# Criss-cross attention and a Fourier mixer: the norm's parts later in each block's iteration, and one small copy on another engine

## The chip, the cores and the metric

The kernel runs on one NeuronCore of a Trainium2 chip. Its engines work from queues of their own: TensorE (PE in the profile, its weight loads PEld), VectorE (DVE), ScalarE (ACT), GpSimd (POOL) and SyncE (SP, which here only starts transfers). An engine takes its instructions in order and waits on semaphores that other engines raise. The metric is the time of one execution in device microseconds, the median of several runs. Before the change it is 3218.33 us (3213.28 to 3226.0 in three runs).

## The reference

The input x has 8 images of 128 x 128 pixels with 64 channels, in fp32. Layer 0 is attention along the column and the row of every pixel, layer 1 a Fourier mixer with a small convolution:

```python
energy_H = jnp.einsum('bhwd,bkwd->bhwk', Q, K)      # Q, K: 8 channels
energy_H = jnp.where(diag, -jnp.inf, energy_H)
energy_W = jnp.einsum('bhwd,bhvd->bhwv', Q, K)
att = jax.nn.softmax(jnp.concatenate([energy_H, energy_W], axis=-1), axis=-1)
x = gamma[0] * (out_H + out_W) + x                  # layer 0
h = _pw(_ln(x, g1, b1), w_te, b_te)                 # layer 1
F = jnp.fft.fft2(h.astype(jnp.complex64), axes=(1, 2))
...
x1 = x + _pw(sp, w_tp, b_tp)
...
return x1 + _pw(d, w_fp, b_fp)
```

The norm that this case speaks of is the first `_ln` of layer 1: mean and variance over the 64 channels of each pixel. The kernel computes it at the end of the attention stage.

## The kernel before, in words

**Stages.** `attention` handles layer 0 for all 8 images and writes for each image the result x2 and the normed, transposed result xn to DRAM. `mixer` reads both and computes layer 1. In the profiled execution the attention stage takes some 1250 of 3220 us; the mixer begins with PE at 1277.

**Blocks.** An image is worked in 8 blocks: four H blocks (32 columns each, attention along the height), then four W blocks (32 rows each, attention along the width). Called H0 to H3 and W0 to W3 here, they make 64 tasks. The loop of line 618 runs over n and is a software pipeline: in iteration n, block n+1 is loaded into PE's layout and gets its queries, keys, values and first energies (to find the maxima), block n gets its shifted energies, exponentials and half of its attend products, and block n-1 the other half. The later work on a W block follows further behind: the weights that merge the two directions (`weigh`, `total`) one iteration after, `invert` and the merge (`combine`) two after, the sums of the norm (`norm_step` with m = n - 4) four after, and the inverse root and the scaling (`norm_step` with m = n - 5, part 3) five after. As an image has four H blocks after the previous image's four W blocks, the norm's sums of an image's W blocks fall into the H iterations of the next image. Those of the last image fall into four iterations after the last block.

**Order.** PE, ACT, DVE and POOL take their instructions in the order in which the loop writes them (`manual_schedule`, line 617). SP's order is made by the framework from the dependencies.

**One iteration on PE:** transposes of block n+1 (L367), attend of n-1 (L422) with the transpose of the maxima (L410), queries and keys (L381), attend of n-1, values (L400), energies of both blocks for two quarters (L452, with mask matmuls L444 in H iterations), values, two attends of n, energies for the other two quarters. All products go to four PSUM buffers of one ring, so each new product waits until an older one has been read: by ACT (xt L371, qt L388, the exponentials L463, the outputs y L428, 128x520 each) or by DVE (shift L411, kt L391, v L403, the negated maxima m L457). Three of the ring's waits matter here: the second pair of energies waits for v, the second values wait for the first maxima, and the next block's transposes for the third maxima.

**The norm's parts.** `norm_step(n, part)` works on half a block (16 rows of 64 channels on 128 partitions, 1024 elements). Part 0 squares the first half on ACT (L578) and sums the rows on DVE (L579); part 1 sums the squares on DVE (L581); parts 2 and 3 do the same for the second half. Part 3 also starts `inverse_root` on POOL for the block before (17 small instructions, lines 88 to 104), and for every second block the scaling of two blocks into `z` (L593, 8 instructions) and the transfer of `z` to xn in DRAM (L597, 2 MB, issued by POOL). Only near the end of the last image do the roots, scalings and squares run on DVE (`merger`; L576).

**The merge.** `combine` is on POOL: 16 instructions of 128x512 (L560 and L563) and the store of x2 (L564). It reads yh, the outputs of the H blocks of its image (one buffer, used for all images), and yw, the outputs of two W blocks (two buffers, `target`, line 489). The squares of part 0 and 2 and `z` are written into the yw buffer of their blocks, so the buffer is free for a later pair only when L597 has read it.

**The maxima.** `maximum(n)` keeps the negated maxima of an H block in `mh` (128x32 of 128x128), which is transposed on PE when the image's H blocks are done (L514); for a W block it starts the weights on POOL (L503). The input was written in the iteration before.

Of the kernel before, what the change touches and what calls it, by code (L numbers as in the profile page):

```python
# [260 lines left out]
def attention(tc, nc, x, w_q, b_q, w_k, b_k, w_v, b_v, gamma, x2, xn, prm, marks, packed, thirds):  # L261
    NB = x.shape[0]
    with ExitStack() as ctx:
# [166 lines left out]
        def energies(a, k, new, old, masked):  # L430


            jobs = []
            if new is not None:
                e1 = ps.tile([P, 2, 4, P], F32, tag="ps", name="e1")
                jobs += [(e1, q, 2 * k + q, new.qt, new.kt, False) for q in range(2)]
            if old is not None:
                e2 = ps.tile([P, 2, 4, P], F32, tag="ps", name="e2")
                jobs += [(e2, q, 2 * (1 - k) + q, old.kt, old.qt, masked) for q in range(2)]
                if masked:  # L440
                    for t in range(4):
                        for q in range(2):
                            rows = slice(32 * (2 * (1 - k) + q), 32 * (2 * (1 - k) + q) + 32)
                            nc.tensor.matmul(  # L444
                                e2[:, q, :, 32 * t : 32 * t + 32], lhsT=mleft[rows, t, :],
                                rhs=mright[rows, :].unsqueeze(1).to_broadcast([32, 4, 32]),
                                start=t == 0, stop=False,
                            )
            for j in range(4):
                for e, q, quad, left, right, msk in jobs:  # L450
                    rows = slice(32 * quad, 32 * quad + 32)
                    nc.tensor.matmul(  # L452
                        e[:, q, j, :], lhsT=left[rows, 4 * a + j, :], rhs=right[rows, 4 * a + j, :],
                        start=not msk, stop=j == 3 or not msk,
                    )
            if new is not None:
                nc.vector.tensor_reduce(  # L457
                    new.mneg[:, 2 * k : 2 * k + 2, 4 * a : 4 * a + 4],
                    e1, AX.X, ALU.max, negate=True,
                )  # L460
            if old is not None:
                att = p4.tile([P, 2, 4, P], F32, tag="att", name="att", bufs=5)
                nc.scalar.activation(att, e2, AF.Exp)  # L463
                old.att[a, 1 - k] = att
# [8 lines left out]
        def begin(n):  # L473
            b, way, blk = tasks[n]
            if way == "H":
                if blk == 0:
                    o = img[b] = Image()
                    o.mh = p2.tile([P, P], F32, tag="mh", name="mh")
                    o.mdt = late.tile([P, 2, P], F32, tag="mdt", name="mdt")
            state[n] = Block(n, loaded.pop(n))  # L480
# [13 lines left out]
        def maximum(n):  # L494

            b, way, blk = tasks[n]
            s, o = state[n], img[b]
            cols = slice(blk * R, blk * R + R)
            if way == "H":
                nc.vector.tensor_copy(o.mh[:, cols].rearrange("p (q i) -> p q i", q=4), s.mneg)  # L500
                return
            t = s.t = late.tile([P, 5, R], F32, tag="tsm", name="tsm", bufs=4)
            nc.gpsimd.tensor_tensor(  # L503
                t[:, 0, :].rearrange("p (q i) -> p q i", q=4),
                o.mdt[:, 0, cols].rearrange("p (q i) -> p q i", q=4), s.mneg, ALU.subtract,
            )
# [12 lines left out]
        def merger(n):  # L519

            return nc.vector if n >= len(tasks) - 3 else nc.gpsimd
# [5 lines left out]
        def is_w(n):  # L527
            return 0 <= n < len(tasks) and tasks[n][1] == "W"
# [37 lines left out]
        def norm_step(n, part):  # L566


            m = n - 4
            if is_w(m):  # L570
                s = state[m]
                h = slice(16 * (part // 2), 16 * (part // 2) + 16)
                sq = s.y[:, h, 0:C]
                if part % 2 == 0:
                    if m >= N - 3:
                        nc.vector.tensor_tensor(sq, s.xb[:, h, :], s.xb[:, h, :], ALU.mult)  # L576
                    else:
                        nc.scalar.activation(sq, s.xb[:, h, :], AF.Square)  # L578
                    nc.vector.tensor_reduce(s.t[:, 0, h], s.xb[:, h, :], AX.X, ALU.add)  # L579
                else:  # L580
                    nc.vector.tensor_reduce(s.t[:, 1, h], sq, AX.X, ALU.add)  # L581
            m = n - 5
            if is_w(m):
                b, way, blk = tasks[m]
                s = state[m]
                r, q, t = (s.t[:, i, :] for i in range(3))
                if part == 3:
                    inverse_root(merger(m), m >= N - 3, r, q, t)
                if part == 3 and blk % 2 == 1:
                    z = s.yw.rearrange("p r c -> p (r c)")[:, 0 : 2 * R * C].rearrange("p (c r) -> p c r", c=C)  # L590
                    for o, lo in ((state[m - 1], 0), (s, R)):
                        for h in range(0, R, 8):
                            merger(m).tensor_tensor(  # L593
                                z[:, :, lo + h : lo + h + 8].rearrange("p c r -> p r c"), o.xb[:, h : h + 8, :],
                                o.t[:, 0, h : h + 8].unsqueeze(2).to_broadcast([P, 8, C]), ALU.mult,
                            )
                    (nc.sync if m >= N - 3 else nc.gpsimd).dma_start(out=xn[b][:, blk // 2, :, :], in_=z)  # L597
# [8 lines left out]
        def flush(n):  # L606
            for _ in range(n):
                if later:
                    later.pop(0)()
# [7 lines left out]
        with tc.manual_schedule(engines={E.PE, E.Activation, E.DVE, E.Pool}):  # L617
            for n in range(-1, N + 6):
                for m in (n + 2, n + 3):
                    if m >= 2 and m < N and (m == n + 2) == (tasks[m][1] == "H"):  # L620
                        fetch(m)
                new = old = last = None
                masked = False
                if n + 1 < N:
                    begin(n + 1)
                    new = state[n + 1]
                    new.turn()
                flush(1)
                if 0 <= n < N:
                    old = state[n]  # L630
                    masked = tasks[n][1] == "H"
                    moved = lambda yp: old.shift(yp[:, 0, 384:512])
                if 0 <= n - 1 < N:
                    last = state[n - 1]
                    last.attend(1, 1, last.y, moved if old is not None else None)
                elif old is not None:
                    moved(ps.tile([P, 2, 512], F32, tag="ps", name="mt"))
                if new is not None:
                    new.queries()
                norm_step(n, 0)  # L640
                if last is not None:
                    last.attend(1, 0, last.y)
                    across_all(n - 1)
                if old is not None:
                    maximum(n)
                if new is not None:
                    new.values(0)
                flush(1)
                norm_step(n, 1)
                if is_w(n - 2):  # L650
                    invert(n - 2)
                if new is not None or old is not None:
                    for k in range(2):
                        energies(0, k, new, old, masked)
                norm_step(n, 2)
                if is_w(n - 1):
                    weigh(n - 1)
                if new is not None:
                    new.values(1)
                if old is not None:  # L660
                    target(n)
                    old.attend(0, 1, old.y)
                    old.attend(0, 0, old.y)
                flush(1)
                if new is not None or old is not None:
                    for k in range(2):
                        energies(1, k, new, old, masked)
                if is_w(n - 1):
                    total(n - 1)
                norm_step(n, 3)  # L670
                if is_w(n - 2):
                    combine(n - 2)
                if 0 <= n < 4:
                    prepare[n]()
                state.pop(n - 7, None)
                flush(1)
# [711 lines left out]
```

## Time and profile before

| | |
|---|---|
| median of three runs | 3218.33 us (3213.28, 3218.33, 3226.0) |
| profiled execution | 3221.41 us, span 3219.6 us |
| busy: PE, PEld, DVE | 2944.8 (91%), 2142.9 (67%), 2548.9 (79%) us |
| busy: ACT, POOL | 2100.1 (65%), 1561.0 (48%) us |
| granted TensorE clock | 0.971 |
| DVE sums of the norm, L579 and L581 | 64 each, median 1207 and 1206 ns |
| ACT squares, L578 | 58, median 1058 ns |
| DVE copy of the maxima, L500 | 32, 169 / 531 / 1159 ns (least, median, most) |
| POOL transfer L597 | 14 of 2048 KB, 9.4 us from issue to landing |

How to read it: busy shares are means over a stage of attention and a stage of mixing with different limits, so what happens in the attention stage is read from its own stretches. In the lines of the prediction, a time line gives the start, the duration in us, the engine, the line of the kernel, the operation, output and inputs, the number of instructions merged, and in brackets the idle time of the engine before it and what ended that. "issue" is idle time for which the profile shows no releaser. The granted clock is a share of TensorE's full clock.

### The profile page before, as it was taken

The numbers are of one execution on the slowest core, as the hardware profiler recorded it, in microseconds if no ns is written. First come the engines' busy times: TensorE is split into PE (matmuls) and PEld (weight loads), VectorE is DVE, ScalarE is ACT, GpSimd is POOL, SyncE is SP. The second block draws the span as 40 slices with busy tenths as digits, with TensorE's granted clock in tenths as the row PEclk, the third lists the DMA queues.
The fourth block names the chain that finished last, engine by engine and source line by source line (L and its number), as shares of the span: only waits on it lengthen the run. The fifth ranks groups of instructions, "written<-read, shape, count | busy, mean of one in ns | idle before, by whom it ended". The sixth has DMA issues, their size and how long they took to land.

```text
span 3219.6 us, 110523 instructions
## 1 busy us (share of the span) xinstructions
PE 2944.8 (91%) x50612; PEld 2142.9 (67%) x50612; DVE 2548.9 (79%) x2322; ACT 2100.1 (65%) x2744; POOL 1561.0 (48%) x1944
## 2 busy tenths in 40 slices
PE   7998888988888987999999899999899999999978
PEld 6877777777777776666576576575566575665644
DVE  4574747474756567719999999999999999999996
ACT  3665656565655655538868768768668678677654
POOL 1095959595958585414515415515415425335321
PEclk8999999999999998999999999999999999999989
DMA  6024242434333323232552653643634634634433
GB/s 174 23 95 129 99 120 95 128 97 136 108 107 120 95 94 135 101 123 40 144 134 50 157 110 66 158 93 73 161 83 89 156 84 93 151 77 81 96 62 75
DMA packets 222458, 339.17 MB, mean 105 GB/s; under 512 B 142879, under 2 KB 176296, under 8 KB 207528
## 3 DMA queue, kind: packets, MB, share of 16 engines
q0 software_dynamic: 32496, 154.84, 20.4%
q1 hardware_dynamic: 188728, 177.19, 19.4%
q8 instruction: 397, 6.50, 0.8%
q14 instruction: 69, 0.57, 0.1%
q10 hardware_dynamic: 768, 0.07, 0.0%
HBM read 137.40 MB, written 102.25 MB: 74 GB/s over the span
## 4 chain that ended last, share of the span: by engine, by line
PE 52%; DVE 33%; issue 6%; POOL 6%; ACT 1%; DMA 1%; SPq 0%; POOLq 0%; DVEq 0%; ACTq 0%
DVE acc L1159 23%; PE yp L422 6%; PE fcps L859 5%; PE e L452 4%; PE dps L927 3%; PE yps L914 3%; PE vps L400 3%; DVE m L457 3%; PE tp L367 3%; PE pq L381 3%; PE yps L916 3%; PE tpy L603 2%; POOL xb L563 2%; PE op L1225 2%; PE aps L819 2%
## 5 line engine op out<-in xcount | busy, mean ns | idle before, releaser
L1159 DVE SCALAR_TENSOR_TENSOR acc<-h,pk,acc 128x1024 f32<-128x1024 f32 x840 | 1332.6, 1591 | 34.8 <-ACT acc L1145 13.3
L875 POOL TENSOR_TENSOR gs<-gl 128x512 f32<-128x512 f32 (+2 forms) x272 | 418.7, 1593 | 245.3 <-ACT gl L869 234.4
L859 PE MATMUL fcps<-f,pk 128*128 128x512 f32 (+2 forms) x1088 | 499.4, 591 | 0.0
L457 DVE TENSOR_REDUCE m<-e 128x8 f32<-128x1024 f32 x256 | 300.9, 1211 | 207.0 <-PE e L452 206.4
L1153 POOL DMA_DIRECT2D acc<-pr x120 | 105.6, 880 | 644.8 <-DVE acc L1159 428.1
L869 ACT ACTIVATE gl<-fcps,pk 128x1024 f32<-128x1024 f32 (+2 forms) x272 | 291.1, 1074 | 118.1 <-PE fcps L859 95.6
L463 ACT ACTIVATE att<-e 128x1024 f32<-128x1024 f32 x256 | 259.7, 1024 | 165.3 <-PE e L452 161.5
L422 PEld LDWEIGHTS yp<-v,att 128*64 128x64 f32 x8192 | 270.3, 143 | 89.1 <-issue 42.2
L1060 POOL TENSOR_TENSOR xc<-x,st 128x512 f32<-128x512 f32 x128 | 183.7, 1440 | 286.5 <-DVE st L101 186.1
L859 PEld LDWEIGHTS fcps<-f,pk 128*128 128x128 f32 x1088 | 190.5, 190 | 197.3 <-issue 162.8
L452 PE MATMUL e<-kt,qt 32*128 32x128 f32 x4096 | 298.4, 288 | 23.8 <-DVE v L403 12.7
L422 PE MATMUL yp<-v,att 128*64 128x65 f32 x8192 | 298.3, 230 | 20.6 <-issue 18.7
L452 PE MATMUL e<-qt,kt 32*128 32x128 f32 x4096 | 297.0, 286 | 15.6 <-issue 13.5
L452 PEld LDWEIGHTS e<-kt,qt 32*128 32x128 f32 x4096 | 257.9, 191 | 44.4 <-issue 21.2
L452 PEld LDWEIGHTS e<-qt,kt 32*128 32x128 f32 x4096 | 255.3, 191 | 20.2 <-issue 13.9
L1149 ACT ACTIVATE pr<-h,pk 128x1024 f32<-128x1024 f32 x176 | 214.1, 1236 | 0.0
L899 PEld LDWEIGHTS gps<-pk,gs 128*64 128x64 f32 x4032 | 135.5, 141 | 116.5 <-issue 65.5
L403 DVE TENSOR_TENSOR v<-vps,bv 128x1024 f32<-128x1024 f32 x128 | 155.9, 1218 | 66.9 <-PE vps L400 66.8
L914 PE MATMUL yps<-tb,gt 128*64 128x128 f32 x1024 | 200.8, 278 | 3.0 <-DVE ot L1230 2.4
L400 PE MATMUL vps<-wv,xt 64*64 64x64 f32 x8192 | 158.9, 228 | 46.6 <-DVE m L457 27.7
L915 PE MATMUL yps<-tb,gt 128*64 128x128 f32 x1024 | 200.8, 278 | 0.0
L842 PE MATMUL fps<-tb,at 128*64 128x128 f32 x1008 | 196.3, 277 | 0.0
(226 smaller groups left out, 7424.5 us busy)
## 6 DMA issues: line engine op xcount, KB each, us to landing
acc<-pr POOLq DMA_DIRECT2D x120, 512.0 KB, 5.4
xb<-in_x_dram SPq DMA_DIRECT2D x32, 1024.0 KB
xn<-xn SPq DMA_DIRECT2D x32, 1024.0 KB
x<-x SPq DMA_DIRECT2D x32, 1024.0 KB
x<-xb POOLq DMA_DIRECT2D x30, 1024.0 KB, 6.0
out_dram<-ot SPq DMA_DIRECT2D x120, 256.0 KB
xn<-yw POOLq DMA_DIRECT2D x14, 2048.0 KB, 9.4
pr<-pr POOLq DMA_DIRECT2D x56, 512.0 KB, 6.4
```

What stands on the lines that cost most here:

```text
L400: nc.tensor.matmul(vps[z, s, j, :], lhsT=self.xts[t][rows, j, z], rhs=wv[rows, :], start=True, stop=True)
L422: nc.tensor.matmul(yq[z, q, j, :], lhsT=att[:, q, j, z], rhs=self.v[:, r, :], start=True, stop=True)
L452: nc.tensor.matmul(e[:, q, j, :], lhsT=left[rows, 4 * a + j, :], rhs=right[rows, 4 * a + j, :], start=not msk, stop=j == 3 or not msk,)
L457: nc.vector.tensor_reduce(new.mneg[:, 2 * k : 2 * k + 2, 4 * a : 4 * a + 4], e1, AX.X, ALU.max, negate=True,)
L463: nc.scalar.activation(att, e2, AF.Exp)
L859: nc.tensor.matmul(ps[:, sgn, 0:n], lhsT=w[:, cols], rhs=fv, start=True, stop=not mean)
L869: nc.scalar.activation(gl[:, :, 0:n], ps[:, :, 0:n], AF.Gelu, bias=bfc[:, half : half + 1])
L875: nc.gpsimd.tensor_tensor(gs[:, 0:n], gl[:, 0, 0:n], gl[:, 1, 0:n], ALU.add if half == 0 else ALU.subtract)
L914: nc.tensor.matmul(yps[0:64, c, :], lhsT=gr, rhs=cosn, start=True, stop=False)
L915: nc.tensor.matmul(yps[64:128, c, :], lhsT=gi, rhs=cosn, start=True, stop=False)
L1149: nc.scalar.activation(pr, self.lines(k, t), AF.Identity, bias=zero, scale=wdw[:, t : t + 1])
L1159: nc.vector.scalar_tensor_tensor(out=a, in0=self.lines(k, t), scalar=wdw[:, t : t + 1], in1=a, op0=ALU.mult, op1=ALU.add)
```

## The change

Part 0 of the norm moves from after the queries to after the first two calls of `energies`, part 1 from before those energies to after the second `values`, and part 2 from before the second `values` to after the last two calls of `energies`. Part 3 stays at the end. In an H iteration the copy of the maxima to `mh` is done by ACT in place of DVE, at the same place of the order.

```diff
             if way == "H":
-                nc.vector.tensor_copy(o.mh[:, cols].rearrange("p (q i) -> p q i", q=4), s.mneg)
+                nc.scalar.copy(o.mh[:, cols].rearrange("p (q i) -> p q i", q=4), s.mneg)
                 return
...
                 if new is not None:
                     new.queries()
-                norm_step(n, 0)
                 if last is not None:
                     last.attend(1, 0, last.y)
                     across_all(n - 1)
...
                 flush(1)
-                norm_step(n, 1)
                 if is_w(n - 2):
                     invert(n - 2)
                 if new is not None or old is not None:
                     for k in range(2):
                         energies(0, k, new, old, masked)
-                norm_step(n, 2)
+                norm_step(n, 0)
                 if is_w(n - 1):
                     weigh(n - 1)
                 if new is not None:
                     new.values(1)
+                norm_step(n, 1)
                 if old is not None:
                     target(n)
                     old.attend(0, 1, old.y)
...
                     for k in range(2):
                         energies(1, k, new, old, masked)
+                norm_step(n, 2)
                 if is_w(n - 1):
                     total(n - 1)
                 norm_step(n, 3)
```

## The prediction

> **What bounds the kernel now.** I read the page first (busy time, shares by slice), then the instructions of single block iterations in order of time, then the chain that ended last, then busy time by stage. The page gives no single bound for the attention stage: TensorE (PE) is busy 7 or 8 tenths in the first sixteen slices, while POOL alternates between full and half.
>
> ```profile
> PE   7998888988888987999999899999899999999978
> POOL 1095959595958585414515415515415425335321
> ```
>
> The block iteration that begins at 350.53 (image 2, second column block, called H1) shows what the change aims at. DVE in order of time:
>
> ```profile
> 355.83 1.23 DVE L391 TENSOR_TENSOR kt<-pq,bk 128x1024 f32<-128x1024 f32 x1 [0.72 <-PE pq L381]
> 356.97 1.21 DVE L579 TENSOR_REDUCE tsm<-xb 128x16 f32<-128x1024 f32 x1
> 358.09 0.88 DVE L500 COPY mh<-m 128x32 f32<-128x32 f32 x1
> 358.90 1.21 DVE L403 TENSOR_TENSOR v<-vps,bv 128x1024 f32<-128x1024 f32 x1
> 360.03 1.20 DVE L581 TENSOR_REDUCE tsm<-yw 128x16 f32<-128x1024 f32 x1
> 361.16 0.34 DVE L547 RECIPROCAL tsm<-tsm 128x32 f32<-128x32 f32 x1
> 361.42 2.28 DVE L457 TENSOR_REDUCE m<-e 128x8 f32<-128x1024 f32 x2
> ```
>
> and PE beside it:
>
> ```profile
> 360.16 0.38 PE L452 MATMUL e<-kt,qt 32*128 32x128 f32 x2 [0.93 <-DVE v L403]
> 362.62 1.16 PE L400 MATMUL vps<-wv,xt 64*64 64x64 f32 x64 [1.29 <-DVE m L457]
> ```
>
> PE stands 0.93 and 1.29 us because v and the maxima queue on DVE behind a norm sum, the copy of the maxima and a second norm sum. So far the change looks worth about 2 us in each of 28 iterations. The chain between two images says otherwise. POOL, from the merge of one image's row blocks (L560, L563) to the transfer of the normed rows (L597):
>
> ```profile
> 312.57 0.25 POOL L541 TENSOR_TENSOR tsm<-mdt,tsm 128x32 f32<-128x32 f32 x1 [12.19 <-ACT tsm L535]
> 404.65 8.12 POOL L593 TENSOR_TENSOR yw<-xb,tsm 128x512 f32<-128x512 f32 x8
> 413.06 0.62 POOL L597 DMA_DIRECT2D xn<-yw  x1 [0.30 <-POOL yw L593]
> ```
>
> and what waits for it on ACT, in images 1, 2 and 5:
>
> ```profile
> 268.98 0.59 ACT L428 COPY yw<-yp 128x520 f32<-128x520 f32 x1 [3.19 <-DMA xn<-yw]
> 422.57 1.09 ACT L428 COPY yw<-yp 128x520 f32<-128x520 f32 x2 [6.71 <-DMA xn<-yw]
> 888.17 0.59 ACT L428 COPY yw<-yp 128x520 f32<-128x520 f32 x1 [4.71 <-DMA xn<-yw]
> ```
>
> POOL's timeline has no gap over 1 us between 312.57 and 413.06: four merges, two inverse roots and one scaling, 100.5 us. The first row block of the next image (W0) writes its outputs into the buffer that this transfer empties (target, line 482, two yw buffers). The page's median landing for L597 is 9.4 us. From its issue to the first W0 copy the seven images take 9.8, 9.5, 13.9, 9.9, 9.7, 12.5 and 9.5 us (issues at 259.17, 413.06, 566.70, 723.15, 878.48, 1032.88, 1189.36). So in five of seven the copy starts as the transfer lands. In images 3 and 6 PE was late instead: 4.84 and 2.29 us of "issue" idle stand before their attend matmuls.
>
> The loop from image to image is then: 12.5 us from the start of W2 to POOL's total, 100.5 on POOL, 9.5 for the transfer, and 31.1 from that copy to the next W2 (453.69): 153.6, which is the distance of the two W2 (300.07 to 453.69). The column blocks H0 to H3, where the change acts, are not in this sum. They run beside POOL:
>
> ```profile
> 332.31:402.77 70.46, 62.84 (x1860) 52.10 (x1861) 56.81 (x54) 45.05 (x56) 64.98 (x93) 1.00 0.31 108
> 402.77:453.69 50.92, 42.43 (x925) 36.04 (x926) 21.49 (x18) 26.59 (x33) 29.25 (x65) 0.93 0.58 168
> ```
>
> (stretch, length, busy PE, PEld, DVE, ACT, POOL, granted clock, DMA share, GB/s; first H0 to H3, then W0 and W1.)
>
> **The change, part by part.** All norm parts act where the block four before is a row block: H0 to H3 of images 1 to 7 (28 iterations), and four iterations after the last block. Parts 0 and 2 are each a Square on ACT (1.06) and a sum on DVE (1.21), part 1 a sum of squares (1.20). None of the three issues anything on POOL or SP and no DMA. Part 3, with the roots, the scaling and L597, stays. So nothing is moved past those two queues.
>
> *Removed from DVE ahead of what PE waits for:* one sum and the copy before v, one sum of squares before the maxima. In the iteration above v could start as its matmuls end, at 357.95 instead of 358.90, and the maxima at 359.3 instead of 361.42. Both idles go: 17.96 - 0.93 - 1.29 = 15.74. An iteration without norm parts is a check: W3 of image 1 takes 15.64, without the column blocks' masks.
>
> *New waits.* (1) The first sum now stands before the second v: DVE from the maxima's end goes 1.21 + 1.21 while PE does vps and two attends (1.16 + 2.09); 0 to 0.3 us. (2) The second Square now stands on ACT between the last exponential and the two xt copies of the next block. The xt copies move back by about 0.85 us; the first has that slack (PE has 3.3 us of other work before the queries), the second not quite: 0.1 to 0.5. (3) A sum and the part-3 sum stand before the shift of qt (L411), which waits for PE until 3.3 us into the iteration; they end at 3.3 us: 0 to 0.1. Together I take 0.3 of 0.1 to 0.9, near the low end since each item has cover: an iteration of 16.0. (4) The copy of the maxima on ACT: no row has ACT doing it; nearest are L533 with 128x32 at 0.22 on ACT and L500 at 0.17 to 1.16 on DVE, so 0.2 to 1.2. I take 0.2, on the same engine; ACT idles 1.04 us just there before the exponential, and without that cover it would cost the 0.2. Its input is an iteration old, so it waits for nothing.
>
> *The sum for H0 to H3.* The seven stretches last 72.60, 70.46, 73.54, 74.43, 72.63, 75.94 and 71.17, mean 73.0, or 18.24 per iteration. Saved: 28 x (18.24 - 16.0) = 63 us on PE. One piece comes back at once: H3's output copy overwrites rows of yh that the merge of W3 still reads, and that merge ends at 397.84 whatever PE does. H3 would reach the copy at about 393.7 and wait until its rows are free, near 395.6, so 2 us of each image go: 63 - 14 = 49.
>
> *What is late next.* W0 would start near 398 instead of 402.77 and reach its first yw copy near 412, where the transfer lands at 422.5 as before. So the wait there grows by what H0 to H3 save, and the end of W0 stays. What can still move is the time after L597's issue. To the start of W2 it is 40.9, 40.6, 42.6, 42.3, 41.4, 43.4 and 38.2. Images 3 and 6, no longer late, go to the mean of the other five (40.7): 1.9 + 2.7 = 4.6 gained. Against this, PE now idles some 10 us before W0's end and resumes at half clock:
>
> ```profile
> 578.90:585.70 6.80, 6.12 (x78) 5.67 (x82) 0.00 (x0) 2.27 (x3) 6.72 (x9) 0.50 0.09 16
> 422.60:427.70 5.10, 4.04 (x75) 3.50 (x74) 2.19 (x2) 3.86 (x5) 4.37 (x12) 1.00 0.41 83
> ```
>
> After the 4.84 us idle of image 3 the clock was 0.50 for 6.8 us; in image 2 it was full after the wait. From the copy to the next block it takes 5.1 and 4.9 us at full clock (images 2 and 5) and 8.0 in image 4 (partly at half). So 3 us each in images 2 and 5 are at risk. Their W1 then holds an "issue" idle of 3.76 and 4.09, during the second pair of transfers, which ends by the transfers and not by PE. I count half: 3. Bounds: 0, and for all seven images a full 6.8 us at half clock, 7 x 3.4 = 24.
>
> The Trainium skill (TensorE: Matmul & The Clock Gate, Part 1) speaks against the change here: it says an idle window of about 3.4 us drops PE to half clock and a busy one restores it. By that rule every W0 would resume cold for one window and lose 1.7 us, 12 in all, if nothing absorbed it.
>
> *After the last block:* the same DVE and ACT instructions in another order. DVE runs without a gap from 1247.33 to 1282, and the mixer's loads wait behind POOL's L503 at 1263.67. Cost 0; without that cover, one Square of 1.06.
>
> *Sum:* -4.6 + 3 + 0 = -1.6 against the profiled execution (span 3219.6, its time 3221.41, 3 above the median of the three runs, 3218.33). On the median: 3217.
>
> **The rivals.** *B, W0 and W1 lose their own stalls too.* If PE, reaching W0 earlier, gets its instructions before the transfers fill the queues, all images could go from L597 to W2 in 38.2, the shortest seen (mean 41.3): 7 x 3.1 = 22, so 3196. For: the idles marked "issue" in W0, and W1, in which the instruction queue (q8, 397 packets, 6.50 MB) is late: in the one from 442.69 to 446.44 its 16 KB packet begins at 443.83. Against: those in W1, like this one, lie under the second transfer, whose time POOL sets. *C, the columns' saving reaches the end:* 3218 - 56 = 3162 (between 49 and 63). It needs a POOL chain that gets shorter with them. Against: that chain runs without a gap, and nothing on it is removed. *D, slower: the cold restart is not absorbed,* up to 24 us: 3242. It decides if PE idles about 5 us or more in W0 and W1 has no slack behind it. For: the half-clock rows. Against: W1's own stalls. *E, the moved parts make H0 to H3 longer:* the second Square before xt, the sums before the shift. It shows only beyond the wait in W0; an iteration would have to grow by over 1 us, about 3230.
>
> **How the numbers follow.** A measurement here tells about 0.5% from no change (the three runs span 0.4%). Forecast 0.64 with its own range 3205 to 3230; B 0.13; C 0.05; D 0.12; E 0.06. The range 3198 to 3238 leaves out C and the far ends of B and D. Below 3202: B and C, 0.18. Above 3234: D and part of E, 0.17. Between: 0.65.
>
> **What would show it.** Right: H0 to H3 fall from 73 to about 66 us, PE's idles before e (L452) and vps (L400) nearly go, while W0 and W1 grow from 49 to about 56, ACT's wait for L597 in W0 reaches 8 to 12 us in every image, and W2 to W2 stays at 153 to 155. Wrong: POOL's chain from L541 to L597 shorter than 100 us, or H0 to H3 no shorter, or another transfer order on SP's queue.

## The result, and the profile after

The changed kernel takes 3206.35 us (median of 22 runs, 3197.29 to 3215.97); beside it the kernel before takes 3212.87 us (22 runs, 3197.09 to 3226.0). The ratio is 0.998, 95% interval 0.9967 to 0.9993. That is inside the 0.5% which the prediction called no change, though the interval ends below 1. The forecast was 3217 us; it was made against three runs of the kernel before with a median of 3218.33, and 5.5 of its 10.7 us of distance are that median's.

The profiled execution of the changed kernel took 3208.46 us, span 3206.3. Its busy shares by slice (TensorE and GpSimd, each digit the tenths of one fortieth of the span):

```profile
PE   7999989898989896999999999899999999999978
POOL 1095959595959585314515515415415425425321
```

GpSimd's row of the attention stage is the old one but for one digit: between full and half by turns. What changed is the inside of the column blocks. VectorE in H1 of image 2, in order of time:

```profile
361.66 1.22 DVE L403 TENSOR_TENSOR v<-vps,bv 128x1024 f32<-128x1024 f32 x1 [0.95 <-PE vps L400]
362.80 0.34 DVE L547 RECIPROCAL tsm<-tsm 128x32 f32<-128x32 f32 x1
363.06 2.31 DVE L457 TENSOR_REDUCE m<-e 128x8 f32<-128x1024 f32 x2
365.29 1.21 DVE L579 TENSOR_REDUCE tsm<-xb 128x16 f32<-128x1024 f32 x1
366.41 1.21 DVE L403 TENSOR_TENSOR v<-vps,bv 128x1024 f32<-128x1024 f32 x1
367.54 1.21 DVE L581 TENSOR_REDUCE tsm<-yw 128x16 f32<-128x1024 f32 x1
```

v (L403) and the maxima (L457) now stand ahead of the norm's sums (L579, L581), and VectorE waits for TensorE, 0.95 us, where TensorE waited for VectorE before. TensorE's second values follow the maxima with 0.16 us of idle in place of 1.29, and ScalarE copies the maxima in 0.22 us:

```profile
364.27 1.34 PE L400 MATMUL vps<-wv,xt 64*64 64x64 f32 x64 [0.16 <-DVE m L457]
361.03 0.22 ACT L500 COPY mh<-m 128x32 f32<-128x32 f32 x1
```

Where the time went is in the same image's stages (stretch, length, busy PE, PEld, DVE, ACT, POOL, granted clock, DMA share, GB/s; first H0 to H3, then W0 and W1):

```profile
337.41:405.78 68.37, 65.56 (x1861) 53.36 (x1861) 54.15 (x49) 44.55 (x59) 63.39 (x86) 1.00 0.28 103
405.78:460.05 54.27, 44.16 (x925) 37.38 (x925) 22.63 (x19) 27.45 (x34) 31.12 (x72) 0.87 0.57 167
```

H0 to H3 went from 70.46 to 68.37 us, W0 and W1 from 50.92 to 54.27. GpSimd's chain to the transfer, and the copies of W0 that wait for it (images 2, 4, 5, 6, 7):

```profile
317.67 0.25 POOL L541 TENSOR_TENSOR tsm<-mdt,tsm 128x32 f32<-128x32 f32 x1 [12.22 <-ACT tsm L535]
409.93 8.12 POOL L593 TENSOR_TENSOR yw<-xb,tsm 128x512 f32<-128x512 f32 x8
418.35 0.62 POOL L597 DMA_DIRECT2D xn<-yw  x1 [0.30 <-POOL yw L593]
```

```profile
427.79 0.59 ACT L428 COPY yw<-yp 128x520 f32<-128x520 f32 x1 [8.36 <-DMA xn<-yw]
736.96 0.59 ACT L428 COPY yw<-yp 128x520 f32<-128x520 f32 x1 [7.36 <-DMA xn<-yw]
889.02 0.59 ACT L428 COPY yw<-yp 128x520 f32<-128x520 f32 x1 [7.43 <-DMA xn<-yw]
1043.91 0.59 ACT L428 COPY yw<-yp 128x520 f32<-128x520 f32 x1 [10.14 <-DMA xn<-yw]
1197.22 0.59 ACT L428 COPY yw<-yp 128x520 f32<-128x520 f32 x1 [7.53 <-DMA xn<-yw]
```

From the start at 317.67 to the issue at 418.35 it is 100.7 us (100.5 before). Images 1 and 3 wait 3.32 and 10.33 us. The sum over the seven images (in the wait before the change, images 3 and 6 are left out, where the copy came after the transfer had landed):

| images 1 to 7, sums in us | before | after |
|---|---|---|
| H0 to H3 | 510.8 | 481.9 |
| W0 | 177.8 | 190.9 |
| W1 | 165.4 | 173.4 |
| ScalarE's wait for L597 before the first copy of W0 | 24.2 | 54.5 |
| issue of L597 to that copy | 74.8 | 66.5 |
| issue of L597 to W2 | 289.4 | 280.2 |
| W2 of image 1 to W2 of image 7 | 927.5 | 918.3 |
| start of the mixer on PE (not a sum) | 1277.3 | 1273.4 |

The columns gave 28.9 us. W0 and W1 together took 21.0 us more, so nearly three quarters of the saving were lost again there. The wait for the transfer grew by 30.3; 10.8 of these are images 3 and 6, where before the change ScalarE idled 6.95 and 3.80 us before that copy for TensorE, and not for the transfer. The chain that ended last says it in another way. Its shares by engine after the change (before: PE 52%, DVE 33%, POOL 6%, DMA 1%):

```profile
PE 43%; DVE 29%; POOL 17%; issue 6%; DMA 3%; ACT 2%; SPq 0%; POOLq 0%; ACTq 0%; DVEq 0%
```

and three of its longer pieces in image 2, from the scaling over the transfer into W0:

```profile
410.93 7.13 POOL yw L593 x7
418.35 9.34 DMA xn<-yw
428.43 3.79 PE e L452 x60
```

Before, the chain was mostly drawn over TensorE and VectorE, and the waits for the transfer were shorter; after, a fifth of it runs over GpSimd and the transfers. The two profiled spans differ by 13.3 us: 3.9 up to the start of the mixer and 9.4 in the mixer, in which nothing was changed (its length was between 1933 and 1942 us in the runs that leave its memory alone). So the attention stage accounts for about 4 us in these two executions, and no edit accounts for the rest. Within it W2 to W2 gained 9.2, and the time before W2 of image 1 lost 5.1, 2.9 of them in H0 to H3 of image 0. These blocks hold none of the norm's sums, and between 71.9 and 84.3 us for them were seen over the kernels of this study.

### The profile page after: what moved, and what is told of

It reads as the page before. It is cut to its first block, busy times and chain, and to the rows that moved or that the text cites. A ratio compares the mean times of both kernels' runs of the same rounds, so it can differ in the third digit from the quotient of the medians.

```text
span 3206.3 us, 110591 instructions
## 1 busy us (share of the span) xinstructions
PE 2967.4 (93%) x50612; PEld 2151.8 (67%) x50612; DVE 2527.0 (79%) x2290; ACT 2104.0 (66%) x2776; POOL 1571.1 (49%) x1944
## 4 chain that ended last, share of the span: by engine, by line
PE 43%; DVE 29%; POOL 17%; issue 6%; DMA 3%; ACT 2%; SPq 0%; POOLq 0%; ACTq 0%; DVEq 0%
DVE acc L1159 22%; POOL xb L563 7%; PE fcps L859 5%; PE dps L927 4%; PE yp L422 3%; PE yps L914 3%; PE e L452 3%; PE yps L916 3%; POOL yh L560 3%; POOL yw L560 3%; PE op L1225 2%; PE aps L819 2%; PE tpy L603 2%; PE vps L400 2%; DMA xn<-yw 2%
## 5 line engine op out<-in xcount | busy, mean ns | idle before, releaser
L1159 DVE SCALAR_TENSOR_TENSOR acc<-h,pk,acc 128x1024 f32<-128x1024 f32 x840 | 1319.1, 1575 | 36.4 <-ACT acc L1145 15.0
L457 DVE TENSOR_REDUCE m<-e 128x8 f32<-128x1024 f32 x256 | 303.2, 1215 | 216.9 <-PE e L452 212.9
L452 PE MATMUL e<-kt,qt 32*128 32x128 f32 x4096 | 308.8, 293 | 12.6 <-issue 7.9
L452 PEld LDWEIGHTS e<-qt,kt 32*128 32x128 f32 x4096 | 262.6, 196 | 40.1 <-ACT yw L428 27.5
L452 PEld LDWEIGHTS e<-kt,qt 32*128 32x128 f32 x4096 | 266.9, 197 | 29.9 <-issue 18.1
L403 DVE TENSOR_TENSOR v<-vps,bv 128x1024 f32<-128x1024 f32 x128 | 156.5, 1223 | 83.3 <-PE vps L400 83.1
L914 PE MATMUL yps<-tb,gt 128*64 128x128 f32 x1024 | 201.9, 279 | 2.6 <-DVE ot L1230 2.0
L915 PE MATMUL yps<-tb,gt 128*64 128x128 f32 x1024 | 201.8, 279 | 0.0
L916 PE MATMUL yps<-tb,gt 128*64 128x128 f32 x1024 | 197.2, 275 | 0.0
L917 PE MATMUL yps<-tb,gt 128*64 128x128 f32 x1024 | 197.2, 275 | 0.0
```

The costliest lines, as they stand in the source:

```text
L452: nc.tensor.matmul(e[:, q, j, :], lhsT=left[rows, 4 * a + j, :], rhs=right[rows, 4 * a + j, :], start=not msk, stop=j == 3 or not msk,)
L457: nc.vector.tensor_reduce(new.mneg[:, 2 * k : 2 * k + 2, 4 * a : 4 * a + 4], e1, AX.X, ALU.max, negate=True,)
L914: nc.tensor.matmul(yps[0:64, c, :], lhsT=gr, rhs=cosn, start=True, stop=False)
L916: nc.tensor.matmul(yps[0:64, c, :], lhsT=gi, rhs=nsinn, start=False, stop=True)
L1159: nc.vector.scalar_tensor_tensor(out=a, in0=self.lines(k, t), scalar=wdw[:, t : t + 1], in1=a, op0=ALU.mult, op1=ALU.add)
```

## The experiments

The theory on record is that GpSimd's chain and its transfer set the distance of the images, so that the columns can give nothing. The main rival: the columns give little because they do not get much shorter, or because something other than the transfer holds W0 and W1. All ratios below are to the kernel before on the same chip.

### Each part alone

`copy_only` is the kernel before with the copy of the maxima on ScalarE:

```diff
-                nc.vector.tensor_copy(o.mh[:, cols].rearrange("p (q i) -> p q i", q=4), s.mneg)
+                nc.scalar.copy(o.mh[:, cols].rearrange("p (q i) -> p q i", q=4), s.mneg)
```

> The kernel before with the copy of the maxima on ACT, the norm's parts left in their places. Theory 1: H0 to H3 lose up to the 0.5 us that the copy takes on DVE, 0 to 2 us per image, W0 waits longer by as much, and the time stays within 8 us of the kernel before. Rival (the copy alone makes the whole gain of 0.2%, since it holds up the value sums at random by up to 1.16 us): H0 to H3 fall by 4 us per image and the time by 6 to 15 us.

Measured: 3207.07 us (10 runs), ratio 0.9976 (0.9958 to 0.9993). `norm_only` is the changed kernel with that copy back on VectorE:

```diff
-                nc.scalar.copy(o.mh[:, cols].rearrange("p (q i) -> p q i", q=4), s.mneg)
+                nc.vector.tensor_copy(o.mh[:, cols].rearrange("p (q i) -> p q i", q=4), s.mneg)
```

> The changed kernel with the copy of the maxima back on DVE: the norm's parts alone are moved. Theory 1: H0 to H3 near 69 us (the copy holds up the value sums by 0 to 0.5 us each), W0's copies again start as the transfer lands, and the time is the changed kernel's, 3206, within 8 us. Rival (the copy makes the whole 0.2%): the time of the kernel before, 3213.

Measured: 3206.43 us (10 runs), ratio 0.9969 (0.9952 to 0.9986). Image 2 of the two (stages as above; `copy_only`, then `norm_only`):

```profile
321.33:392.46 71.13, 63.50 (x1861) 52.82 (x1861) 54.82 (x50) 45.33 (x59) 65.49 (x95) 0.99 0.29 107
392.46:444.62 52.16, 44.17 (x927) 37.64 (x926) 21.44 (x18) 26.74 (x33) 28.70 (x63) 0.89 0.57 163
```

```profile
327.86:393.54 65.68, 64.19 (x1860) 52.50 (x1860) 56.71 (x52) 43.93 (x54) 61.43 (x79) 1.00 0.27 100
393.54:449.73 56.19, 43.36 (x928) 36.27 (x925) 22.69 (x19) 27.49 (x34) 33.04 (x78) 0.88 0.57 170
```

The copy alone shortens H0 to H3 over seven images from 510.8 to 499.3 us, or 0.41 us for each of 28 iterations; the moved sums alone shorten them to 471.1. (With both it is 481.9, so single profiles differ by some 10 us in this sum.) W0 and W1 give it back: 353.3 and 375.3 us against 343.2. Both kernels end where the whole change ends. By its time alone `copy_only`, 6.2 us below the kernel before on its chip, meets both forecasts; its columns, 1.6 us shorter in each image and not 4, speak against the rival. So the parts don't add up, which fits a wait behind them that absorbs what they save. The 0.2% that is left comes with either part, and no run shows where from.

### GpSimd's chain made longer

`after_newton5` is the changed kernel with two more Newton steps in each inverse root on GpSimd; it adds work, and the computation is otherwise the same.

```diff
-    for _ in range(3):
+    for _ in range(3 if fused else 5):
```

> The changed kernel with five Newton steps in place of three in the inverse roots on POOL: 8 instructions of about 0.35 us more per root, two roots between L541 and L597, so 5.5 us more in POOL's chain of each image and nothing more for PE, ACT or DVE. Theory 1: 7 x 5.5 = 38 us slower than the changed kernel, chain L541 to L597 106 us. Theory 2 (POOL is hidden): within 8 us of the changed kernel.

Measured: 3223.98 us (10 runs), ratio 1.0039 (1.0015 to 1.0062), 17.6 us above the changed kernel. The chain from L541 to the issue is 105.9 us, 5.3 longer. Image 2, and the copy that waits:

```profile
336.60:405.40 68.80, 65.08 (x1860) 53.26 (x1860) 54.03 (x48) 44.30 (x58) 63.60 (x88) 0.99 0.26 95
405.40:459.90 54.50, 43.08 (x928) 37.01 (x925) 22.77 (x19) 27.87 (x34) 38.75 (x102) 0.89 0.59 173
```

```profile
422.73 0.62 POOL L597 DMA_DIRECT2D xn<-yw  x1 [0.30 <-POOL yw L593]
431.72 1.09 ACT L428 COPY yw<-yp 128x520 f32<-128x520 f32 x2 [12.16 <-POOL tsm L103]
```

(The bracket of the copy names an old GpSimd instruction; it starts 9.0 us after the issue, when the transfer lands.) H0 to H3 is the same, and the wait in W0 grew from 8.36 to 12.16. W0 over seven images grew from 190.9 to 229.9 us. So what GpSimd adds shows in the wait, though half of the 38 us expected did not reach the end: W1 fell from 173.4 to 160.0, by 13 us. W1 had time to give back, which the sum of the prediction's loop had put at none. In the changed kernel the loop over GpSimd binds, but not rigidly.

### The wait taken away, first two arrangements

A third buffer for the merged rows lets W0 write while the transfer still reads. Room for it comes from the weights' buffers (`att`, three in place of five); in the profiles of the last pair with this edit, `before_yw3c` and `after_yw3c`, the exponentials that write them wait for TensorE's energies alone. The same edit in the changed kernel (`after_yw3`) and in the kernel before (`before_yw3`):

```diff
-    flat = lambda: pool.tile([P, 2 * R, C + 1], F32, tag="yw", name="pk").rearrange("p r c -> p (r c)")
+    flat = lambda: pool.tile([P, 2 * R, C + 1], F32, tag="yw", name="pk", bufs=3).rearrange("p r c -> p (r c)")
...
-                att = p4.tile([P, 2, 4, P], F32, tag="att", name="att", bufs=5)
+                att = p4.tile([P, 2, 4, P], F32, tag="att", name="att", bufs=3)
...
-                    o.yw = late.tile([P, 2 * R, C + 1], F32, tag="yw", name="yw")
+                    o.yw = late.tile([P, 2 * R, C + 1], F32, tag="yw", name="yw", bufs=3)
```

> The changed kernel with a third yw buffer (and three in place of five att buffers, to make room). Theory 1, the loop through POOL and the transfer L597 takes up what H0 to H3 save: the first copy of W0 no longer waits for the transfer, the 29 us saved in H0 to H3 and the waits in W0 (7 to 10 us of ACT's idle in each image) come through, 10 to 14 us per image: 70 to 98 us less than the changed kernel, about 3110 to 3135. W0 falls from 27 to about 21 us. Theory 2, the saving is lost on PE itself in W0 and W1 (late instructions, transposes of yh): W0 and W1 stay at 52 us together, the time within 15 us of the changed kernel.

> The kernel before with the same third yw buffer. Theory 1: the wait goes here too, but H0 to H3 stay at 73 us, so only 3 to 7 us per image come through: 20 to 50 us less than before, and the distance to the changed kernel with three buffers is what H0 to H3 save, 29 us or more. Theory 2: within 15 us of the kernel before, and 6 us from the changed one with three buffers.

Measured: `after_yw3` 3189.43 us (4 runs), ratio 0.9924 (0.9894 to 0.9954); `before_yw3` 3258.65 us (4 runs), ratio 1.0131 (1.0102 to 1.016). The changed kernel's attention stage gained: the mixer starts at 1196.5 us, 77 earlier, and H0 to H3, W0 and W1 sum to 469.3, 150.7 and 151.9. In the kernel before the same edit moved that start by 4.5 us only, to 1272.8: its copies in W0 start 4 to 6.5 us after the issue in six images, without the wait, but W0 and W1 still take 49.7 us an image, with idles marked "issue" in them.

Both lost some 50 us in the mixer's first image (219 us against 168), a loss that neither expectation had, and both missed. The waits of `after_yw3` between 1180 and 1290 us (engine, line, what it waited for: us in total, times, longest):

```profile
ACT f L849 <- DMA xn<-yw: 49.3, 1, 49.3
POOL gs L875 <- ACT gl L869: 80.4, 7, 64.5
```

The mixer's tile f lies over memory that the attention stage's larger set of buffers now takes, and ScalarE stands 49.3 us until the last transfer has read it. So the edit changed two things at once, and the time of either kernel by itself says nothing on the wait. Their distance says more, as the layout is the same in both: 69 us, and in the profiles H0 to H3 are 30.3 us shorter in the changed kernel, W0 and W1 45.5.

The second pair put one of the six W input buffers ahead of the third yw buffer in memory, and left five where they were (`after_yw3b`, `before_yw3b`; the three lines above, and):

```diff
+        xone = ctx.enter_context(tc.tile_pool(name="a_xone", bufs=1))
...
-        xw = ctx.enter_context(tc.tile_pool(name="a_xw", bufs=6))
+        xw = ctx.enter_context(tc.tile_pool(name="a_xw", bufs=5))
...
-                xb = xw.tile([P, R, C], F32, tag="xw", name="xb")
+                pool = xone if (4 * b + blk) % 6 == 2 else xw
+                xb = pool.tile([P, R, C], F32, tag="xw", name="xb")
```

> The changed kernel with the third yw buffer, and one of the six W input buffers placed ahead of the late tiles, so that the mixer's first tiles lie over the same early-dead memory as in the changed kernel. Theory 1 (the loop over POOL and the transfer hid the gain; the 51 us that the mixer's first image lost with three buffers came from the memory layout alone): the mixer begins near 1200, its first image takes 168 us again, 50 us less than the first version with three buffers: about 3140. Theory 2 (the mixer's first image is slower because it begins ahead of the tail of the last blocks, whatever the layout): its first image stays near 219 us, the time near 3190.

> The kernel before with the same buffers and layout. With the layout's 51 us gone: 3205 to 3215, within 8 us of the kernel before, although no copy waits for the transfer: its H0 to H3 end when the transfers run, and PE then stands in W0 and W1 for late instructions (issue idles of 2 to 4 us), 49 us for both as before. The distance to the changed kernel with the same buffers: 60 to 75 us. If the wait for the buffer were all that held the kernel before: 25 us or more below it.

Measured: `after_yw3b` 3181.46 us (7 runs), ratio 0.9905 (0.9875 to 0.9935); `before_yw3b` 3247.78 us (4 runs), ratio 1.0105 (1.0065 to 1.0146). Both missed the times that were expected, though their distance of 66 us is inside the expected 60 to 75 (H0 to H3 are 30.4 us shorter in the changed kernel, W0 and W1 38.1). The collision moved and did not go:

```profile
POOL gs L877 <- DVE yw L595: 53.5, 1, 53.5
```

GpSimd's gs now waits 53.5 us for the last scaling, and the first image of the mixer takes 205 us in both. The attention stage of `after_yw3b` shows in image 2 what W0 and W1 are without the wait:

```profile
323.23:389.00 65.77, 64.28 (x1860) 52.49 (x1860) 54.13 (x48) 44.34 (x58) 61.52 (x79) 1.00 0.27 99
389.00:430.97 41.97, 39.88 (x928) 33.36 (x925) 22.69 (x19) 27.86 (x34) 32.99 (x78) 1.00 0.63 192
```

That is 41.97 us for W0 and W1 in place of 54.27, at full clock, with the same TensorE work.

### The wait taken away, without the loss in the mixer

The third pair keeps the order in memory at the mixer's first tiles: two W input buffers ahead of the yw buffers, four behind, and the second H input buffer at the end (`after_yw3c`, `before_yw3c`; the three lines of the first pair, and):

```diff
-        xh = ctx.enter_context(tc.tile_pool(name="a_xh", bufs=2))
...
+        xh = [ctx.enter_context(tc.tile_pool(name="a_xh", bufs=1))]
+        xtwo = ctx.enter_context(tc.tile_pool(name="a_xtwo", bufs=2))
...
-        xw = ctx.enter_context(tc.tile_pool(name="a_xw", bufs=6))
+        xw = ctx.enter_context(tc.tile_pool(name="a_xw", bufs=4))
+        xh.append(ctx.enter_context(tc.tile_pool(name="a_xh2", bufs=1)))
...
-                xb = xh.tile([P, R, C], F32, tag="xh", name="xb")
+                xb = xh[blk % 2].tile([P, R, C], F32, tag="xh", name="xb")
...
-                xb = xw.tile([P, R, C], F32, tag="xw", name="xb")
+                pool = xtwo if (4 * b + blk) % 6 in (2, 3) else xw
+                xb = pool.tile([P, R, C], F32, tag="xw", name="xb")
```

> The changed kernel with three yw buffers, arranged so that neither the mixer's first tiles (f, gl) nor its gs tiles lie over memory that the last blocks still use: two of the six W input buffers stand ahead of the late tiles, the second H input buffer at the end. If the mixer's loss in its first image (37 us in the second arrangement, where POOL's gs stood 53.5 us for a scaling on DVE) is a matter of layout: first image 168 us, mixer 1935 to 1942, attention as in the second arrangement, mixer from about 1195: 3135 to 3150. If not: 3180 as before.

> The kernel before in the same arrangement. Attention as in its second arrangement (W0 and W1 about 48 us by late instructions, mixer from about 1261), the mixer at 1940: 3200 to 3212, 0 to 14 us below the kernel before; the changed kernel in this arrangement is 55 to 70 us faster, which is what H0 to H3 save when the transfer's buffer no longer holds W0.

Measured: `after_yw3c` 3159.15 us (6 runs, 3139.72 to 3177.38), ratio 0.9824 (0.979 to 0.9859); `before_yw3c` 3205.84 us (10 runs), ratio 0.9981 (0.9961 to 1.0). The mixer's first image takes 169 us in both, so the loss in the mixer is gone, and no copy of yw waits for the transfer any more. What ScalarE waited for before the copies of yh and yw in `after_yw3c` (all the releasers; L431 is the copy here):

```profile
  PE yp L425: 122.0, 144
  DVE qt L414: 82.5, 63
  POOL xb L566: 2.6, 3
```

This is the test of the theory. With the wait the change is worth 6.5 us between medians, without it 47 (3205.84 to 3159.15). That is short of the 55 to 70 that were expected; `before_yw3c` lies in its range, `after_yw3c` 9 us above its own. In the profiled executions, which are 35 us apart, 32 lie before the mixer, 27 in H0 to H3 of images 1 to 7. So in all three pairs what H0 to H3 save, 27 to 30 us, reaches the end when no copy waits. What W0 and W1 add to it differs, 45.5, 38.1 and 1.9 us, and no run shows why.

The wait alone is worth 7 us in the kernel before, which is inside the noise. From W2 of image 1 to W2 of image 7 `before_yw3c` takes 924.1 us, and with the wait it is 927.5. So in the kernel before GpSimd's loop is not the only bound: TensorE's own path, with its idles marked "issue", is nearly as long. Only both edits together pay.

The third arrangement also lost something. In its profiled execution the mixer begins at 1235.3 us, where 1195 was expected and `after_yw3b` had 1194.7; W0 and W1 sum to 340.5 us over seven images, where `after_yw3b` had 299.2. So these two executions, 3170.22 and 3173.67 us, are nearly equal, though the medians are 22 us apart. `after_yw3c` is the fastest kernel of the study, 1.8% below the kernel before and 47 us below the changed one.

It is not free of stalls. Image 2 and image 6 of `after_yw3c` (first H0 to H3, then W0 and W1):

```profile
322.99:392.64 69.65, 65.93 (x1861) 54.08 (x1861) 54.16 (x49) 44.53 (x59) 64.41 (x90) 0.98 0.29 108
392.64:445.24 52.60, 43.77 (x924) 36.88 (x925) 22.63 (x19) 27.59 (x34) 30.04 (x68) 0.90 0.57 163
...
934.81:1001.07 66.26, 64.00 (x1861) 52.38 (x1861) 54.08 (x49) 44.43 (x59) 61.72 (x80) 1.00 0.27 99
1001.07:1043.90 42.83, 39.72 (x925) 33.49 (x926) 22.55 (x19) 27.70 (x34) 32.79 (x78) 1.00 0.65 200
```

W0 and W1 of image 2 take 10 us more than those of image 6, with no wait for the transfer in either. In image 2 TensorE stands at idles marked "issue". The same holds for the kernel before: between 170 and 1217 us of `before_yw3c` its TensorE waited

```profile
PE e L455 <- issue: 20.0, 13, 3.1
PE vps L403 <- issue: 15.3, 9, 2.4
PE yp L425 <- issue: 13.4, 5, 4.0
```

48.7 us in 27 idles.

### The transfers held back

These idles fall mostly where 2 MB transfers and the loads of the next W blocks fill the DMA engines: of 41 us of them in the changed kernel (counted in the last section), 30 lie in W0 and W1, and between 404 and 430 us, in W0 of image 2, the two queues took 31.1% and 35.1% of the 16 engines' time. To part the two, the first pair's transfer was held until the second pair's, which the third buffer allows (`before_yw3b_defer` is `before_yw3b` with this, `after_yw3c_defer` is `after_yw3c` with it):

```diff
+        waiting = []
...
-                    (nc.sync if m >= N - 3 else nc.gpsimd).dma_start(out=xn[b][:, blk // 2, :, :], in_=z)
+                    waiting.append((xn[b][:, blk // 2, :, :], z))
+                    if blk == 3:
+                        for dst, src in waiting:
+                            (nc.sync if m >= N - 3 else nc.gpsimd).dma_start(out=dst, in_=src)
+                        waiting.clear()
```

> The kernel before with three yw buffers, and the transfer of the first two W blocks held back until that of the other two, so that POOL issues both 21 us later, one after the other. If the transfers make PE's instructions late in W0 and W1: the issue idles of 2 us and more in W0 fall away or shrink, W0 from about 25 to 21 us, and W1 and W2 get them instead (W1 25 us or more, W2 over 16.6). If the idles have another cause: W0 and W1 as without the delay, about 25 us each.

> The changed kernel with three yw buffers in the third arrangement, and the transfer of the first two W blocks held back until that of the other two. If PE's late instructions in W0 come from that transfer: W0 near 21 us in every image (25 in five of seven before), W1 takes part of it back; 5 to 25 us below the same kernel without the delay (3159), 3135 to 3155. If the loads of the W inputs, which are not moved, make them late, or W1 and W2 lose what W0 gains: 3150 to 3170, no difference that can be told.

Measured: `before_yw3b_defer` 3244.39 us (10 runs), ratio 1.0092 (1.007 to 1.0114), against 1.0105 without the delay; `after_yw3c_defer` 3162.1 us (4 runs), ratio 0.9862 (0.9826 to 0.9897), against 0.9824. Neither differs from its own kernel. In the profiles W0 got shorter, from 176.6 to 156.3 us over seven images in the first and from 170.3 to 157.1 in the second; W1 went from 160.7 to 168.2, and from 170.2 to 169.4. TensorE's "issue" idles in `after_yw3c_defer` still sum to 42.1 us between 240 and 1230 us, against 47.8 without the delay. (The profiled execution of `before_yw3b_defer`, 3211.08 us, was the lowest of its ten, 33 us below their median, so its stages flatter it; that of `after_yw3c` was 11 us above its own.) So the transfer in W0 may be part of the cause, which single executions that far apart don't show, and it is not the whole of it. The loads of the W blocks were not moved, and what share is theirs stays open.

## Why the prediction was right, and where its terms were not

**The wait absorbs the saving: shown.** The step "the wait there grows by what H0 to H3 save, and the end of W0 stays" is what the trace has in the main: 28.9 us saved, 21.0 of them taken back in W0 and W1, where the wait for the transfer is 30.3 us longer (19.5 with all of ScalarE's idle before that copy on both sides). Where the wait is taken away with another buffer, the saving reaches the end (47 us); where GpSimd's chain gets longer, the wait grows, and half of what was added reaches the end. The chain was 100.7 us in image 2, W2 to W2 153.0 us on average (148.7 to 154.9; 153 to 155 foretold), the wait 7.4 to 10.3 us in six images and 3.3 in the first (8 to 12 foretold in every one). One step of the argument is weak: that 12.5, 100.5, 9.5 and 31.1 us add up to the distance of the two W2 shows nothing, since they are consecutive times of one trace. What bears the loop is that the copy starts as the transfer lands, and the pairs above, which also show that the kernel before has a second bound nearly as long.

**The saving in H0 to H3: too large.** An iteration was put at 16.0 us from 18.24, or 63 us in all. The shortest two took 15.94 and ten of 28 at most 16.5, but the median is 16.7 and the mean 17.2, since some wait for their instructions (the longest, 21.3, 20.1 and 19.5). So the saving was 28.9. The step "H3's output copy waits for rows that the merge of W3 still reads", 14 us, did not come: ScalarE's copies of yh waited 2.2 us for GpSimd in all seven images together, 0.8 at most. The net of the two steps, 49, is near the 47 of the third pair by luck: the pair's columns differ by 27 us. Of the other 20, 12 are the distance of the profiled executions from their medians (`after_yw3c` was profiled 11 us above its own), 5 lie elsewhere in the attention stage and 3 behind it. "H0 to H3 fall from 73 to about 66" became 68.8, "W0 and W1 grow from 49 to about 56" 52.0.

**Images 3 and 6 no longer late: right.** The term was -4.6 us up to W2, and there the two gained 5.3 (42.6 and 43.4 to 40.2 and 40.6). The time from the issue to the first copy is 9.2 to 9.7 us in all seven images, where it was 12.5 and 13.9 in two, and sums to 8.3 us less.

**The cold restart: about the size counted, in other images.** The step was "3 us each in images 2 and 5 are at risk", counted half with +3. TensorE did resume at half clock after the wait. TensorE at work just after it, in images 2 to 7 (granted clock in the third column from the end):

```profile
428.40:433.30 4.90, 4.87 (x66) 4.64 (x67) 2.26 (x2) 3.46 (x4) 4.32 (x11) 0.50 0.36 72
583.50:586.90 3.40, 3.36 (x58) 3.36 (x60) 1.23 (x1) 2.49 (x3) 2.85 (x9) 0.50 0.40 80
737.60:741.00 3.40, 3.39 (x61) 3.27 (x61) 1.23 (x1) 2.46 (x3) 2.82 (x9) 0.57 0.47 97
889.60:893.00 3.40, 3.23 (x66) 2.92 (x67) 2.05 (x2) 3.06 (x5) 2.83 (x9) 1.00 0.44 89
1044.50:1048.00 3.50, 3.45 (x60) 3.36 (x60) 1.22 (x1) 2.50 (x4) 2.98 (x9) 0.54 0.40 80
1197.90:1201.30 3.40, 3.40 (x60) 3.40 (x60) 1.23 (x1) 2.41 (x3) 2.75 (x10) 0.50 0.59 115
```

In five of the six it is 0.50 to 0.57; TensorE had stood still for 3.8 to 7.2 us before it in four of these, and for 2.0 and 2.3 us, one soon after the other, in image 7. Image 5, where it had stood for 0.7 us, is at full clock. From the copy to W1 TensorE has the same 68 matmuls in each of the six. Image 5 takes 4.33 us for them, the others 5.90, 5.35, 5.13, 5.23 and 5.38: 1.07 us more on average, 5.3 in all. In `after_newton5`, whose TensorE has the same instructions, image 2 is at half clock all through this stretch (first image 5 of the changed kernel, then this):

```profile
889.02:893.35 4.33, 3.58 (x68) 3.27 (x69) 2.40 (x2) 3.98 (x5) 3.59 (x12) 1.00 0.49 101
431.72:437.86 6.14, 5.49 (x68) 5.27 (x69) 2.45 (x2) 4.12 (x5) 4.82 (x20) 0.50 0.48 93
```

That is 1.8 us more. So the restart costs 0.8 to 1.8 us where it comes, and +3 in all was of the right size, though image 5, one of the two it was put in, had none. Whether the 5.3 us reach the end is not shown: from the issue to W2 the seven images gained 9.2 us all the same. The 8.0 us of image 4 that the risk was taken from were for the most part an idle of TensorE from 731.87 to 735.28, marked "issue", and not the clock. The rule of the Trainium skill (TensorE: Matmul & The Clock Gate, Part 1), which the prediction set against the change, agrees with four of these rows on the drop to half clock after an idle window, and image 7 is not far from it. The 12 us that were worked out from it, an estimate, are more than twice what is measured.

**Rivals.** B asked that issue to W2 falls to 38.2 us in every image; it fell from a mean of 41.3 to 40.0, mostly by the lateness above. C, the saving at the end, is what the pairs with a third buffer make of it, and not what the change does. D, a restart of up to 24 us, did not come: 5.3 are seen. E, longer columns, neither: they got shorter.

**The sum.** -4.6 + 3 + 0 stands against -9.2 from W2 of image 1 to W2 of image 7, and -3.9 up to the mixer. The forecast lay 0.3% above the result. That the time came out so near does not by itself speak for the mechanism, since columns that save nothing would have given it too; the rows of H0 to H3 and the pairs do.

## What to carry to other kernels

Before costing a saving, close the loop: add up one round of the chain that returns to the same wait, and see whether the edited stretch is in the sum. That the times add up proves nothing, so lengthen the chain or take its wait away, and measure that. A stretch that is not in the round gave next to nothing by itself here, however busy its engine looked, but what it saved came through once the wait was taken away, and the wait alone was worth little too. The two edits should be tried together. When a buffer is added to take a wait away, look also at the first waits of the next stage, since its tiles may have lain over the memory that moved.

## What the runs showed of the hardware

- **TensorE's late instructions stand at one place of every 256.** In the trace of the changed kernel, between 240 and 1215 us, 21 times more than 1.5 us pass from the start of one of TensorE's weight loads to the start of the next. Five are the end of the wait for the transfer. Of the other 16 (41 us in all, 1.6 to 4.4 each), every one falls where the count of TensorE's instructions (weight loads, matmuls and its semaphore instructions) is 193 or 194 modulo 256, and at each a 16 KB packet of the instruction queue (q8) ends 1.2 to 1.7 us before the next load begins. The 19 of the kernel before fall there too. These idles are what the page calls "issue". In the 3 us before each of these 16 packets began, transfers and loads took at least 76% of the time of the 16 DMA engines; before at least half of that queue's other 165 packets in this stretch it was none. That one packet holds 256 of these instructions is read from these positions, and was not tested by itself.
- **VectorE's small copy beside GpSimd varies, ScalarE's does not.** The same 128x32 copy in fp32 took 169 to 1159 ns on VectorE (median 531) and 208 to 239 on ScalarE. On VectorE the four copies of image 0, where GpSimd did nothing, took 170 to 173 ns. GpSimd was at work for at least 94% of each of the 18 that took over 300, though some took 170 beside it too.
- **Half the clock cost less than twice the time.** For the same 68 matmuls, with the waits between them, TensorE took 4.33 us at full clock and 6.14 at 0.50; it was busy for 3.58 and 5.49 us of them.
